# Attention score passes on one core: keys and queries fetched for several heads at once, shifts written by one DMA, their parts made on VectorE

## The chip, the cores and the metric

The kernel runs on one core of a Trainium2 chip. Its time is the device time of one execution in microseconds (us). Before the change it is 2822.1 us, the median of three runs (2809.25 to 2826.09). Lower is better.

A core has five engines that take their instructions in order and wait for each other through semaphores: TensorE (PE, with its weight loads listed as PEld), VectorE (DVE), ScalarE (ACT), GpSimd (POOL) and SyncE (SP). SP computes nothing here. It issues nearly all DMAs.

## The reference, cut to what matters

The input is `x` of shape 4 x 2048 x 256 in float32. Two pre-norm layers follow each other, each with attention and a feed-forward part. The change touches the attention of the second layer, which has 16 heads of 16 channels, rotary positions and a causal mask:

```
Q, K, V = (proj(W_Q), proj(W_K), proj(W_V))
Q = _apply_rope(Q, cos, sin)
K = _apply_rope(K, cos, sin)
scores = jnp.einsum('bhsd,bhtd->bhst', Q, K) / jnp.sqrt(jnp.float32(D_K))
causal = jnp.tril(jnp.ones((S, S), dtype=bool))
scores = jnp.where(causal[None, None], scores, -jnp.inf)
attn = jax.nn.softmax(scores, axis=-1)
out = jnp.einsum('bhst,bhtd->bhsd', attn, V)
```

The first layer's attention has one head of 64 channels. Its feed-forward part is one product with weights rounded to fp8. The second layer's feed-forward part mixes each token with the one before it and has three 256 x 256 products.

## The kernel before, in words

**Tiles.** The 4 x 2048 tokens are cut into 16 blocks of 512 tokens (`BLK`), four per sequence. The 16 heads are taken in 4 groups of 4 (`HG`). A round is one block of queries with one group: 64 rounds. For the block with place `qb` in its sequence a round runs over `qb + 1` blocks of keys, which makes 160 pairs of round and key block in all.

**Two score passes per round.** A head has 16 channels. Query and key are each split into a high and a low part, and four products of them are stacked, so that a score matmul contracts over 64 rows (`QR`), plus 12 rows (`SR`) for the shifts. Pass D (`d_head`, L1043) computes scores with queries on the output's partitions, and DVE takes the row maxima (L792, and L788 on the diagonal block, which adds the mask). Pass E (`e_head`, L1101) computes the transposed scores, and ACT takes the exponential (L1119). The row maximum is subtracted inside the matmul: its negative is split into three bf16 parts, which stand in the 12 extra rows of the query tile `q`; the extra rows of the keys' tile `ke` hold ones in the three rows of the head and zeros elsewhere. In pass D the extra rows of `kd` are zero. `values` (L1127) then multiplies the exponentials with the values.

**From the maxima to the shifts** (`shifts`). When the last D unit of a round is done, DVE reduces the maxima (L1058, tile `sm`), `bf16_parts` makes the three parts with four small operations on POOL (L747 to L750, tile `mp`), TensorE transposes them (L761), ACT copies the result into tile `m` (L766), and four DMAs, one for each head, write the 12 rows of `m` into the head's query tile (L1067). The first layer's attention uses `bf16_parts` too, 16 times, so that it runs 80 times.

**Where keys and queries come from.** `l1_qkv` writes rotated queries and keys to DRAM (L991). `fetch` (L949) loads one head of one block, 64 rows of 2 KB (128 KB), into a buffer: `kd` for pass D (6 buffers), `ke0` to `ke3` for pass E (2 for each place in the group), `q` for queries (12 buffers, which is three rounds). The value blocks `v1` are loaded by L1079.

**The order of the work.** It isn't written out by hand. `Plan.op` takes each operation with its engine, a cost in ns, and what it reads and writes; `Plan.run` is a list planner that gives every operation a start by these costs, picks the PSUM bank or buffer for each result, and emits the program in that order, for each engine. `LAT` is the delay that it adds when an operation on that engine needs the result of another engine. A DMA is planned with 500 ns of issue on SP, 1300 ns until it moves data, its own cost (390 for a key fetch) and 700 ns to the end. The pace of D against E is set by `target`, and the other layers' parts (`l0_attention`, `l0_ffn`, `l1_qkv`, `l1_out`, `l1_ffn`) fill in between by due times. SP takes its DMAs in that order too, so a DMA that waits for a buffer holds all DMAs behind it. All 8 PSUM banks are one class, `ps`. Where TensorE would idle at the beginning and the end, the planner puts `warm` matmuls (L1466) that keep its clock up.

**Costs in the plan that the change names.** The four operations of `bf16_parts` count 1080 ns on POOL. The mixing of tokens in `l1_ffn` (L1209, two per half) counts 661 ns on DVE.

Of the kernel before, what the change touches and what calls it, by code (L numbers as in the profile page):

```python
# [23 lines left out]
P = 128  # L24
C = 256
CK = C // P
BLK = 512
# [35 lines left out]
LAT = {"ACT": 38.0, "DVE": 38.0, "PE": 55.0, "POOL": 68.0, "SP": 60.0}  # L63
# [8 lines left out]
class Plan:  # L72
# [50 lines left out]
    def run(self, key):  # L123
# [54 lines left out]
        while len(done) < total:  # L178
# [75 lines left out]
            if e == "SP":  # L254
                eng_free[e] = s + 500.0
                begin = max(s + 1300.0, dma_end[0])
                dma_end[0] = begin + o.occ
                o.finish = begin + o.occ + 700.0
            else:
                eng_free[e] = s + o.occ  # L260
                o.finish = s + o.lat
# [6 lines left out]
            for b in o.bufs:  # L268
# [11 lines left out]
                if b.left == 0:  # L280
                    free[b.cls][b.slot] = b.end + 55.0
# [100 lines left out]
def seq_kernel(  # L382
# [45 lines left out]
        "kd": (6, [QR + SR, BLK], F32R),  # L428
        **{f"ke{h}": (2, [QR + SR, BLK], F32R) for h in range(HG)},
        "q": (12, [QR + SR, BLK], F32R),  # L430
# [54 lines left out]
    for z, t in enumerate(tiles["q"] + tiles["kd"]):  # L485
        (nc.vector.tensor_copy, nc.scalar.copy)[z % 2](t[QR : QR + SR, :], none)
# [53 lines left out]
    def ready_ke(h):  # L540
# [11 lines left out]
        for t in tiles[f"ke{h}"]:  # L552
            nc.gpsimd.tensor_copy(
                t[QR : QR + SR, :].rearrange("p (a n) -> p a n", n=P),
# [186 lines left out]
    def bf16_parts(nm, n, mp, view, s):  # L741

        def f():
# [3 lines left out]
            nc.gpsimd.tensor_copy(o(0), v3(v))  # L747
            nc.gpsimd.tensor_tensor(v3(r), v3(v), o(0), ALU.subtract)
            nc.gpsimd.tensor_copy(o(1), v3(r))
            nc.gpsimd.tensor_tensor(o(2), v3(r), o(1), ALU.subtract)  # L750
        def v3(a):
            return a.rearrange("p (t h) -> p t h", t=TT)
        op("POOL", 1080.0, f, r=[has["l0" if n == TT else "l1"]], rw=[nm], w=[mp], stream=s)
# [193 lines left out]
    def fetch(cls, name, what, i, head, s):  # L947
        b = buf(cls, name)
        op("SP", 390.0, lambda: nc.sync.dma_start(  # L949
            T_(b)[:QR, :].bitcast(F32),  # L950
            rot_t[what][i][head * 8 : head * 8 + 8].rearrange("d c n -> (d c) n")), r=[rot[what][i]], w=[b], stream=s,
           off=OFF_FETCH)
# [72 lines left out]
    def d_units(i, g, Qs):  # L1025
# [3 lines left out]
        for kb in range(qb + 1):  # L1029
            Ks = [fetch("kd", f"kd_{tag}_{kb}_{h}", "k", i - qb + kb, g * HG + h, now[0])  # L1030
                  for h in range(HG)]
            for t in range(TT) if kb < qb else reversed(range(TT)):
                u = Unit()
                u.kb, u.t, u.diag, u.w, u.mx = kb, t, kb == qb, BLK if kb < qb else (t + 1) * P, mx
                u.Ks, u.Qs, u.r = Ks, Qs, (i, g)
# [4 lines left out]
    def d_head(u, h, s):  # L1040

        def f():
            nc.tensor.matmul(  # L1043
                T_(u.banks[h])[:, : u.w], T_(u.Qs[h])[:, u.t * P : (u.t + 1) * P],
                T_(u.Ks[h])[:, : u.w], start=True, stop=True,
# [492 lines left out]
```

## Time and profile before

| | |
|---|---|
| median of three runs | 2822.1 us (2809.25 to 2826.09) |
| profiled execution | 2808.66 us, of it 2806.9 us span |
| mean granted clock of TensorE | 0.985 |
| busy: PE, DVE, ACT, POOL | 2739.7, 1945.0, 1638.8, 693.4 us |
| DMA | 417.33 MB, 49.6% of 16 engines' time in the queue that SP feeds |
| DMA issues on SP: kd, ke, q, shifts | 640, 640, 256, 256 |
| median length of one such issue | 546, 547, 588, 756 ns |

In the lists of groups a line gives the source line, engine, operation, written and read tiles with shapes, and the count; behind the first bar the busy time in us and the mean ns of one; behind the second the idle time of the engine just before them and what ended most of it. In the chain that ended last each step goes back to what released it. SPq and PEldq are the sequencers of SP and of TensorE's weight loads: they issue DMAs and wait for semaphores. Where a line has "min/median/max", these are ns.

### The profile page before, as it was taken

How to read it: one execution, taken by the hardware profiler on the slowest of the kernel's cores; microseconds unless marked ns; L12 is line 12 of the kernel's file. 1: busy time of each engine (PE TensorE's matmuls, PEld its weight loads, DVE VectorE, ACT ScalarE, POOL GpSimd, SP SyncE). 2: the span in 40 equal slices, each digit the busy share in tenths (PEclk: the TensorE clock that was granted, in tenths of full speed). 3: DMA queues.
4: the chain of work that ended last, by engine and by line, in shares of the span. 5: the costliest groups of instructions: out<-in, count | busy, mean ns of one | idle time of the engine just before them, and what ended most of it. 6: DMA issues, size and time to landing. Idle time of an engine off the chain costs nothing.

```text
span 2806.9 us, 47871 instructions
## 1 busy us (share of the span) xinstructions
PE 2739.7 (98%) x15447; PEld 1655.1 (59%) x15550; DVE 1945.0 (69%) x5040; ACT 1638.8 (58%) x3163; POOL 693.4 (25%) x955
## 2 busy tenths in 40 slices
PE   9999999999999999999999999999999999999998
PEld 5555665565656565655565656566565566555564
DVE  4567688787646778777674678867765477777871
ACT  3345566556565656656666456655666555655665
POOL 4551124013113313212113132501221422120000
PEclk9999999999999999999999999999999999999999
DMA  3664546444446564634544565644454645454331
GB/s 93 192 211 130 173 128 201 131 123 153 126 127 211 153 189 139 193 110 131 162 146 141 167 189 157 188 143 123 124 156 118 192 151 177 148 175 130 108 100 38
DMA packets 275291, 417.33 MB, mean 149 GB/s; under 512 B 42657, under 2 KB 108898, under 8 KB 275042
## 3 DMA queue, kind: packets, MB, share of 16 engines
q1 hardware_dynamic: 273568, 413.57, 49.6%
q8 instruction: 126, 2.06, 0.3%
q14 instruction: 123, 1.01, 0.1%
q10 hardware_dynamic: 1474, 0.69, 0.1%
HBM read 294.56 MB, written 100.66 MB: 141 GB/s over the span
## 4 chain that ended last, share of the span: by engine, by line
PE 81%; DMA 7%; DVE 5%; issue 2%; ACT 2%; POOL 2%; SPq 1%; POOLq 0%; ACTq 0%; DVEq 0%
PE ps L1043 18%; PE ps L1101 17%; PE ps L1127 16%; PE ps L708 9%; PE ps L715 6%; PE ps L894 3%; DMA kd<-k 3%; PE ps L798 2%; DVE mx L792 2%; PE ps L689 1%; DVE ps L788 1%; PE ps L882 1%; PE ps L850 1%; PE ps L903 1%; PE ps L851 1%
## 5 line engine op out<-in xcount | busy, mean ns | idle before, releaser
L1119 ACT ACTIVATE p<-ps 128x512 f32<-128x512 f32 (+1 forms) x2240 | 1188.9, 598 | 649.5 <-PE ps L1101 386.3
L792 DVE TENSOR_REDUCE mx<-ps 128x1 f32<-128x512 f32 x1632 | 1030.2, 683 | 285.1 <-PE ps L1043 260.7
L1043 PE MATMUL ps<-kd,q 76*128 76x512 f32 (+3 forms) x2560 | 1007.7, 419 | 26.3 <-DMA kd<-k 12.6
L1101 PE MATMUL ps<-q,ke 76*128 76x512 f32 (+3 forms) x2560 | 955.3, 401 | 12.6 <-DMA q<-m 3.8
L788 DVE CUSTOM_DVE_ANT_0 ps<-ps,dmask 128x128 f32<-128x128 f32 (+3 forms) x1088 | 507.1, 517 | 257.0 <-PE ps L1043 246.8
L1043 PEld LDWEIGHTS ps<-kd,q 76*128 76x128 f32 x2560 | 481.1, 193 | 246.8 <-issue 87.4
L1101 PEld LDWEIGHTS ps<-q,ke 76*128 76x128 f32 x2560 | 477.3, 191 | 200.3 <-issue 77.6
L1127 PE MATMUL ps<-p,v 128*32 128x512 f32 (+3 forms) x5120 | 541.6, 540 | 1.1 <-DVE mx L792 0.8
L1127 PEld LDWEIGHTS ps<-p,v 128*32 128x32 f32 x5120 | 135.0, 110 | 256.8 <-issue 235.0
L708 PE MATMUL ps<-wb,W 128*128 128x256 f32 x768 | 187.2, 388 | 0.2
L638 POOL TENSOR_SCALAR sm<-sm 128x4 f32<-128x4 f32 x64 | 15.4, 241 | 670.2 <-DVE sm L632 647.9
L798 PE MATMUL ps<-maskT_b,ident_b 128*128 128x128 bf16 (+2 forms) x721 | 177.7, 246 | 0.4
L708 PEld LDWEIGHTS ps<-wb,W 128*128 128x128 f32 x768 | 145.9, 194 | 24.0 <-ACT p L1119 1.0
L788 DVE DVE_READ_ACCUMULATOR2_ANT mx<- 128x1 f32 x1088 | 153.7, 141 | 0.0
L798 PEld LDWEIGHTS <-ident_b 128*128 128x128 bf16 x768 | 75.9, 99 | 120.5 <-issue 103.5
L894 PE MATMUL ps<-p,v 128*65 128x512 f32 (+3 forms) x320 | 145.0, 540 | 1.3 <-ACT p L889 0.7
L774 POOL TENSOR_TENSOR r<-w,r 128x512 fp32r<-128x512 f32 x80 | 103.4, 1296 | 107.0 <-DVE r L773 89.9
L660 ACT ACTIVATE w<-x,sm 128x256 f32<-128x256 f32 x192 | 105.6, 604 | 34.7 <-DVE sm L645 20.3
L979 POOL TENSOR_TENSOR w<-w,cs 128x512 f32<-128x512 f32 x64 | 86.3, 1348 | 158.9 <-ACT w L972 150.5
L889 ACT ACTIVATE p<-ps 128x512 f32<-128x512 f32 (+3 forms) x160 | 86.2, 540 | 67.2 <-PE ps L798 18.8
L738 POOL TENSOR_TENSOR x<-x,w 128x512 f32<-128x512 f32 x32 | 41.1, 1286 | 331.7 <-DVE w L1235 324.5
L715 PE MATMUL ps<-W,wa 128*128 128x512 f32 x256 | 121.8, 599 | 0.7 <-DMA wa<-in_wqk1T 0.5
(123 smaller groups left out, 2515.8 us busy)
## 6 DMA issues: line engine op xcount, KB each, us to landing
kd<-k SPq DMA_DIRECT2D x640, 128.0 KB
ke<-k SPq DMA_DIRECT2D x640, 128.0 KB
k<-r SPq DMA_DIRECT2D x128, 256.0 KB
q<-r SPq DMA_DIRECT2D x128, 256.0 KB
q<-q SPq DMA_DIRECT2D x256, 128.0 KB
v<-v SPq DMA_DIRECT2D x160, 136.0 KB
x<-mid SPq DMA_DIRECT2D x62, 256.0 KB
v<-vs SPq DMA_DIRECT2D x16, 544.0 KB
```

What stands on the lines that cost most here:

```text
L660: nc.scalar.activation(d, T_(x)[:, t, :], AF.Identity, bias=m[:, 16 + t : 17 + t], scale=m[:, 8 + t : 9 + t],)
L708: nc.tensor.matmul(dst, lhsT[:, k, t * P : (t + 1) * P], w[:, k, :], start=(k == 0), stop=(k == CK - 1),)
L715: nc.tensor.matmul(dst, w[:, k, c0 : c0 + P], xT[:, k, :], start=(k == 0), stop=(k == CK - 1))
L774: op("POOL", pool2(BLK), lambda: nc.gpsimd.tensor_tensor(T_(lo), T_(f32), T_(hi), ALU.subtract), r=[f32, hi], w=[lo], stream=s)
L788: nc.vector.tensor_tensor_reduce(a, a, dmask[:, BLK - w :], 1.0, LOW, ALU.add, ALU.max, out())
L792: nc.vector.reduce_max(out(), a, axis=AX.X)
L798: nc.tensor.matmul(o, ident_b, maskT_b[:, 0, :] if len(o.shape) == 2 else maskT_b[:, : o.shape[1], :], start=False, stop=True,)
L894: nc.tensor.matmul(T_(acc)[: D0 + 1, c0:], T_(V_)[:, kt % TT, :], T_(p)[:, c0:], start=(kt == 0), stop=(kt == nkt - 1),)
L1043: nc.tensor.matmul(T_(u.banks[h])[:, : u.w], T_(u.Qs[h])[:, u.t * P : (u.t + 1) * P], T_(u.Ks[h])[:, : u.w], start=True, stop=True,)
L1101: nc.tensor.matmul(T_(u.banks[j])[:, c : c + u.w], T_(u.Ks[h])[:, u.t * P : (u.t + 1) * P], T_(u.Qs[h])[:, u.c0 :], start=h % u.n == 0, st ...
L1119: op("ACT", act(u.n * u.w), lambda: nc.scalar.activation(T_(u.ps[j])[:, c0:], T_(u.banks[j])[:, c0:], AF.Exp, scale=DK**-0.5), r=[u.banks[ ...
L1127: nc.tensor.matmul(T_(acc)[h * 32 : (h + 1) * 32, u.c0 :], T_(u.V)[:, (u.t * HG + h) * VW : (u.t * HG + h) * VW + 32], T_(u.ps[h // u.n])[ ...
```

## The change

Per key block, pass D has two fetches of two heads each (`kd`: 3 buffers of two heads) where it had four of one, and pass E has one fetch of four heads (`ke`: 2 buffers of four heads). Queries come with one fetch of four heads (`q`: 3 buffers of four heads). The space that the buffers take is the same, and so are the bytes moved. The 12 shift rows go into all four heads' places by one DMA whose source is read four times. The four operations that make the parts run on DVE, planned at 320 ns. Some of the planner's constants differ: the delay towards TensorE is 165 instead of 55 and also counts when a PSUM bank comes free; a DMA issue counts 600, the time until it moves data 1900; a fetch counts 390 per head, the shift DMA 200; L1209 counts 950.

```diff
-LAT = {"ACT": 38.0, "DVE": 38.0, "PE": 55.0, "POOL": 68.0, "SP": 60.0}
+LAT = {"ACT": 38.0, "DVE": 38.0, "PE": 165.0, "POOL": 68.0, "SP": 60.0}
...
-                eng_free[e] = s + 500.0
-                begin = max(s + 1300.0, dma_end[0])
+                eng_free[e] = s + 600.0
+                begin = max(s + 1900.0, dma_end[0])
...
-                    free[b.cls][b.slot] = b.end + 55.0
+                    free[b.cls][b.slot] = b.end + (LAT["PE"] if b.cls == "ps" else 55.0)
...
-        "kd": (6, [QR + SR, BLK], F32R),
-        **{f"ke{h}": (2, [QR + SR, BLK], F32R) for h in range(HG)},
-        "q": (12, [QR + SR, BLK], F32R),
+        "kd": (3, [QR + SR, 2, BLK], F32R),
+        "ke": (2, [QR + SR, HG, BLK], F32R),
+        "q": (3, [QR + SR, HG, BLK], F32R),
...
-            nc.gpsimd.tensor_copy(o(0), v3(v))
-            nc.gpsimd.tensor_tensor(v3(r), v3(v), o(0), ALU.subtract)
-            nc.gpsimd.tensor_copy(o(1), v3(r))
-            nc.gpsimd.tensor_tensor(o(2), v3(r), o(1), ALU.subtract)
+            nc.vector.tensor_copy(o(0), v3(v))
+            nc.vector.tensor_tensor(v3(r), v3(v), o(0), ALU.subtract)
+            nc.vector.tensor_copy(o(1), v3(r))
+            nc.vector.tensor_tensor(o(2), v3(r), o(1), ALU.subtract)
...
-        op("POOL", 1080.0, f, r=[has["l0" if n == TT else "l1"]], rw=[nm], w=[mp], stream=s)
+        op("DVE", 320.0, f, r=[has["l0" if n == TT else "l1"]], rw=[nm], w=[mp], stream=s)
...
-    def fetch(cls, name, what, i, head, s):
+    def fetch(cls, name, what, i, head, n, s):
+
         b = buf(cls, name)
-        op("SP", 390.0, lambda: nc.sync.dma_start(
-            T_(b)[:QR, :].bitcast(F32),
-            rot_t[what][i][head * 8 : head * 8 + 8].rearrange("d c n -> (d c) n")), r=[rot[what][i]], w=[b], stream=s,
-           off=OFF_FETCH)
+        op("SP", 390.0 * n, lambda: nc.sync.dma_start(
+            T_(b)[:QR].bitcast(F32),
+            rot_t[what][i][head * 8 : (head + n) * 8].rearrange("(h d) c n -> (d c) h n", h=n)),
+           r=[rot[what][i]], w=[b], stream=s, off=OFF_FETCH)
...
-            Ks = [fetch("kd", f"kd_{tag}_{kb}_{h}", "k", i - qb + kb, g * HG + h, now[0])
-                  for h in range(HG)]
+            Ks = [fetch("kd", f"kd_{tag}_{kb}_{z}", "k", i - qb + kb, g * HG + 2 * z, 2, now[0])
+                  for z in range(2)]
...
-        for h in range(HG):
-            op("SP", 100.0, lambda h=h: nc.sync.dma_start(
-                T_(u.Qs[h])[rows, :].bitcast(F32), T_(m)[rows, :].bitcast(F32)),
-               r=[m], w=[u.Qs[h]], stream=s)
+        op("SP", 200.0, lambda: nc.sync.dma_start(
+            T_(u.Q)[rows].bitcast(F32),
+            T_(m)[rows, None, :].to_broadcast([SR, HG, BLK]).bitcast(F32)), r=[m], w=[u.Q], stream=s)
...
-            Ks = [fetch(f"ke{h}", f"ke_{tag}_{kb}_{h}", "k", i - qb + kb, g * HG + h, now[0])
-                  for h in range(HG)]
+            K = fetch("ke", f"ke_{tag}_{kb}", "k", i - qb + kb, g * HG, HG, now[0])
...
-                op("DVE", 661.0, lambda k=k, d=d, z=z: nc.vector.scalar_tensor_tensor(
+                op("DVE", 950.0, lambda k=k, d=d, z=z: nc.vector.scalar_tensor_tensor(
...
-            Qs = queries[i, g] = [
-                fetch("q", f"q_{i}_{g}_{h}", "q", i, g * HG + h, now[0]) for h in range(HG)]
+            Qs = queries[i, g] = fetch("q", f"q_{i}_{g}", "q", i, g * HG, HG, now[0])
```

The matmuls read the head's part of the wider tiles (`T_(u.K)[:, h, ...]`, `T_(u.Ks[h // 2])[:, h % 2, ...]`, `T_(u.Q)[:, h, ...]`). Below the changed lines the source lines move by one or two: L1043 becomes L1045, L792 L793, L788 L789, L761 L762, L747 to L750 become L748 to L751, L949 becomes L951, L1067 L1068, L1058 L1060.

More of the change, by code (lines that the diff above doesn't have):

```diff
@@ L484, in seq_kernel @@
     nc.vector.memset(none, 0.0)
-    for z, t in enumerate(tiles["q"] + tiles["kd"]):
-        (nc.vector.tensor_copy, nc.scalar.copy)[z % 2](t[QR : QR + SR, :], none)
+    for t in tiles["q"] + tiles["kd"]:
+        for h in range(t.shape[1]):
+            (nc.vector.tensor_copy, nc.scalar.copy)[h % 2](t[QR : QR + SR, h, :], none)
     wo0 = const.tile([D0 + 1, C + 1], F32, name="wo0")
@@ L551, in ready_ke @@
         )
-        for t in tiles[f"ke{h}"]:
+        for t in tiles["ke"]:
             nc.gpsimd.tensor_copy(
-                t[QR : QR + SR, :].rearrange("p (a n) -> p a n", n=P),
+                t[QR : QR + SR, h, :].rearrange("p (a n) -> p a n", n=P),
                 r[:, None, :].to_broadcast([SR, BLK // P, P]),
@@ L1034, in d_units @@
                 u.kb, u.t, u.diag, u.w, u.mx = kb, t, kb == qb, BLK if kb < qb else (t + 1) * P, mx
-                u.Ks, u.Qs, u.r = Ks, Qs, (i, g)
+                u.Ks, u.Q, u.r = Ks, Qs, (i, g)
                 u.banks = [bank(f"d_{tag}_{kb}_{t}_{h}") for h in range(HG)]
@@ L1043, in f @@
             nc.tensor.matmul(
-                T_(u.banks[h])[:, : u.w], T_(u.Qs[h])[:, u.t * P : (u.t + 1) * P],
-                T_(u.Ks[h])[:, : u.w], start=True, stop=True,
+                T_(u.banks[h])[:, : u.w], T_(u.Q)[:, h, u.t * P : (u.t + 1) * P],
+                T_(u.Ks[h // 2])[:, h % 2, : u.w], start=True, stop=True,
             )
-        o = pe(f, max(pass_(u.w), LOADS), end=pass_(u.w), r=[u.Qs[h], u.Ks[h]], w=[u.banks[h], u.mx], stream=s)
+        o = pe(f, max(pass_(u.w), LOADS), end=pass_(u.w), r=[u.Q, u.Ks[h // 2]], w=[u.banks[h], u.mx], stream=s)
         chain(("d", h), o)
@@ L1085, in e_units @@
                 u.w = BLK - u.c0
-                u.Ks, u.V, u.Qs = Ks, V, Qs
+                u.K, u.V, u.Q = K, V, Qs
                 u.first, u.last = kb == qb and t == 0, kb == kbs[-1] and t == TT - 1
@@ L1101, in f @@
             nc.tensor.matmul(
-                T_(u.banks[j])[:, c : c + u.w], T_(u.Ks[h])[:, u.t * P : (u.t + 1) * P],
-                T_(u.Qs[h])[:, u.c0 :], start=h % u.n == 0, stop=not u.diag,
+                T_(u.banks[j])[:, c : c + u.w], T_(u.K)[:, h, u.t * P : (u.t + 1) * P],
+                T_(u.Q)[:, h, u.c0 :], start=h % u.n == 0, stop=not u.diag,
             )
@@ L1111, in e_head @@
             occ, end = max(pass_(u.w), LOADS), pass_(u.w)
-        o = pe(f, occ, end=end, r=[u.Qs[h], u.Ks[h], has["ke"]], w=[u.banks[j], u.ps[j]], stream=s)
+        o = pe(f, occ, end=end, r=[u.Q, u.K, has["ke"]], w=[u.banks[j], u.ps[j]], stream=s)
         chain(("e", h), o)
```

## The prediction

> **What bounds the kernel now.** I read the page's first two parts first, then its chain, then its groups. The profiled execution took 2808.66 us: 2806.9 us of span and 1.8 us around it. The median of the runs shown, 2822.1, lies 13.4 us above it.
>
> ```profile
> PE 2739.7 (98%) x15447; PEld 1655.1 (59%) x15550; DVE 1945.0 (69%) x5040; ACT 1638.8 (58%) x3163; POOL 693.4 (25%) x955
> ...
> PE  9999999999999999999999999999999999999998
> ...
> PE 81%; DMA 7%; DVE 5%; issue 2%; ACT 2%; POOL 2%; SPq 1%; POOLq 0%; ACTq 0%; DVEq 0%
> ...
> L1043 PE MATMUL ps<-kd,q 76*128 76x512 f32 (+3 forms) x2560 | 1007.7, 419 | 26.3 <-DMA kd<-k 12.6
> L1101 PE MATMUL ps<-q,ke 76*128 76x512 f32 (+3 forms) x2560 | 955.3, 401 | 12.6 <-DMA q<-m 3.8
> ```
>
> TensorE is busy in every slice, and its visible idle time is 2806.9 - 2739.7 = 67.2 us. The change removes no matmul, so all it can gain is stall time, and all it can lose is new stall time. The two groups are the score passes that the change feeds: L1043 (for the row maxima, "D") and L1101 (for the exponentials, "E"). "Busy" hides some more stall: in the trace the starts of two such 512-column matmuls are 230 ns apart when nothing holds them, while one record lasts about 395 ns, so a hold of up to 165 ns leaves no idle time. The mean of the 512-column form, 453 ns at L1043 and 431 at L1101, shows that there are such holds.
>
> Next the answers for tile q (idle time of TensorE and of its weight loads, and what ended it) and for lines L1043 and L1101 (duration min/median/max in ns).
>
> ```profile
>   DMA kd<-k: 13.5, 21
> ...
>   DMA q<-m: 8.4, 21
> ...
>   DMA q<-q: 5.7, 11
> ...
>   DMA ke<-k: 5.0, 6
> ```
> ```profile
> L1043 PEldq EVENT_SEMAPHORE  x551: 51/51/1990, 121.3 to 2723.7; - x184
> ```
> ```profile
> L1101 PEldq EVENT_SEMAPHORE  x510: 51/51/2780, 149.1 to 2761.2; - x170
> ```
>
> TensorE waits for data 32.6 us in the first four rows. The last two rows are separate wait instructions on TensorE's sequencer: one stands ahead of an instruction that has more than one semaphore to wait for.
>
> **The change, part by part.** Where I count "PE work", I took the instructions of TensorE in the program's order, before and changed, and gave each its usual start-to-start time in this trace (230 ns for 512 columns of a score pass, 176 for 384, 1.85 us for the 16 records of a values block, and so on). The list of both programs gives the same matmuls; only 12 more clock-warming ones (222 to 234).
>
> *Key fetches of D (kd, 640 of 128 KB to 320 of 256 KB).* The number of buffers' bytes is the same, so what counts is the PE work between the last reader of a buffer and the first reader of its next contents. Before, it is under 3 us for 27 of 634 refills and under 4 us for 51; changed, for 1 and 21 of 317 (the planner's DMA lead went from 1300 to 1900). Adding up what is missing to a need of N us, once per key block, N = 3.0 gives 11.8 us and 3.25 gives 16.9 for the program before: the measured 12.6 to 13.5 us fit N = 3.1. That agrees with the landing marks: a kd fetch lands 2.9 us (median) after its issue. What a 256 KB fetch of this pattern needs is not in the trace. Nearest rows: 256 KB of w<-con land in 2.73 us, 256 KB of x<-mid in 4.32. So N lies between 2.9 and 4.5, and the changed stall between 1.7 and 26 us. I take +0.35 us (four more 2 KB packets per DMA engine, median 84 ns each), N = 3.45: 3 us. Gain 10 us, range 12 gained to 13 lost.
>
> A rule is weighed here: the Trainium skill, "DMA: Bandwidth & Descriptors", section "Anatomy of one DMA", gives about 2.0 us plus bytes / 436 GB/s, so that 256 KB would cost only 0.3 us more than 128 KB. By it the stall would be about 3 us, by the row of x<-mid, which lands 1.4 us after a kd fetch would, about 26.
>
> *Key fetches of E (ke, 640 to 160) and queries (q, 256 to 64).* PE work between use and reuse of a ke buffer is never under 7.5 us, before or changed, so the ke wait stays or goes (5.0 to 0; I count 0). For q, the smallest spacing goes from 1.5 us to 4.5; 544 KB (v<-vs) land in 3.96 us, 0.9 more than a q fetch's 3.03, so N is 4.0 and nothing waits. Gain 4 us of the 5.7, range 0 to 5.7.
>
> *The shifts (four q<-m issues to one).* The last round shows the cost, in the chain of waits and in the row of the line:
>
> ```profile
> 2737.87 0.19 SPq L1067
> 2738.05 0.05 issue
> 2738.11 0.77 SPq L1067
> 2738.87 0.05 issue
> 2738.93 0.71 SPq L1067
> 2739.64 0.04 issue
> 2739.68 2.07 DMA q<-m
> ```
> ```profile
> L1067 SPq DMA_DIRECT2D q<-m x256: 713/756/1503, 147.0 to 2739.7; - x128
> ```
>
> Head 3 is written three issues, 2.4 us, after head 0, while TensorE uses it some 1.4 us later: the last head decides. One issue with the same landing saves about 1 us in a round that is tight. PE work between the transposes of the shifts (L761) and the first E matmul is also a little wider (5th percentile 3.7 to 4.4 us). Gain 5 us of the 8.4. If the one issue takes as long as four (3.0 us), nothing is gained: range 0 to 8.4. SP issues 1184 DMAs less (some 0.55 us each, 0.76 for shifts: about 690 us of its time). That matters only through the waits above, since SP mostly waits for TensorE to free buffers.
>
> *Fewer semaphores for TensorE.* With one buffer for four heads only the first reader must wait for its DMA. Score matmuls with a DMA wait go from 1174 to 475, instructions with two or more waits from 1191 to 596. Price of one: the row says 51 ns of the sequencer, which runs ahead, so 0 to 51 ns, 0 to 30 us in all. Starts of neighbouring score matmuls with such a wait between them lie 20 to 27 ns further apart on average than those without. 595 x 20 is 12 us, some of it DMA wait that is counted above: gain 9 us.
>
> *Parts of the shifts on DVE instead of POOL (4 x 80 small operations).* On POOL they took 1.11 us from first start to last end. This is the last round:
>
> ```profile
> 2735.03 0.22 POOL L747 CAST mp<-sm 128x16 bf16<-128x16 f32 x1 [1.38 <-PE ps L1101]
> ...
> 2735.91 0.23 POOL L750 TENSOR_TENSOR mp<-sm,mp 128x16 bf16<-128x16 f32 x1
> 2736.20 0.26 PEld L761 LDWEIGHTS <-mp 128*76 128x76 bf16 x4 [0.55 <-POOL mp L750]
> ```
>
> The nearest DVE rows are L632 (128x2, 182 ns) and L1058 (128x16, 175 to 217), and a DVE operation that needs the one before starts 30 ns after its end (L631 to L632 in the tail). Four make about 0.8 us. The planner now counts 320 ns where it counted 1080, and has moved L761 up by about 0.6 us (smallest PE work from the last D matmul to L761: 1.8 to 1.26 us); the chain shrinks by 0.3 us plus the 0.3 us handover to POOL. So L761 waits as it does now: 0, give or take 3. But the next row maxima queue behind the parts: 0.8 us on DVE 80 times, of which 0.32 is planned, so up to 0.48 x 80 = 38 us if each delay reached TensorE through a late PSUM bank. DVE is 69% busy and about one reuse of a bank in ten has no slack: loss 4 us, range 0 to 38.
>
> *The planner's other constants.* A larger lead from an engine to TensorE (55 to 165) would pay if it moved matmuls away from banks just released. It did not: the PE work between two writes of a bank after a 512-column D matmul is 1470 ns at the 5th percentile and 2.96 to 2.98 us at the median, before and changed. I count 0. Switches between the fast and the four-pass matmuls go from 1685 to 1655; a score matmul's interval is 316 ns instead of 230 ahead of one: gain 3 us. In the tail, after the last E matmul, stand 63 warming matmuls instead of 53; those ahead of L715 (24 for 19, 214 ns each) and of the last L708 (4 for 1) delay real work: loss 1.5 us, range 0 to 2.
>
> **Sum:** -10 - 4 - 5 - 9 + 4 - 3 + 1.5 = -25.5 us, so 2783 us for the profiled execution, 0.9% less. On the median of 2822.1 this is **2797 us**.
>
> **Rivals.** (A) *Much faster*: the multi-wait instructions cost their whole 51 ns and the DMA waits vanish: -30 - 12 - 5.7 - 8.4 - 3 = -59, 2763 us. For it: means of 453 and 431 ns show holds that no idle time tells. Against it: the sequencer runs ahead, and most intervals with such a wait are the ordinary 230 ns. (B) *No change*: the larger fetch lands like x<-mid (+13 us) and eats the rest: about -25 + 23 = -2 us, 2820. For it: that row. Against it: w<-con, just as large, lands in 2.73 us. This is also the case in which the change only moves issue time on SP, whose queue is not what TensorE waits for. (C) *Slower*: DVE turns into the bound at the round boundaries. Each of the 80 sets of parts stands in DVE's order ahead of row maxima that free PSUM banks. If the four operations take 1.1 us as on POOL (0.78 more than planned) and TensorE feels all of it, 0.78 x 80 = 62 us are lost against the 29.5 of the other terms: +33 us, 2855. It turns the sign from 29.5 / 80 = 0.37 us of new stall per set. For it: D's matmuls wait for banks that DVE frees already (29.7 and 22.2 us of idle time in the answer for tile kd are ended by L792 and L788). Against it: DVE is idle 31% of the time.
>
> **How the numbers follow.** Forecast (15 to 40 us gained) 0.49, A 0.17, B 0.19, C 0.15. About 1% (28 us) is what a measurement of this kernel can tell from no change, since its three runs spread over 17 us; half of the forecast's band is beyond it. Faster: 0.25 + 0.17 = 0.42. Slower: 0.12, as C with only two thirds of its delay stays within 1%. Same: the other half of the forecast, B and the rest of C, 0.46. The range reaches from A (2763, and a few us less for runs as fast as the profiled one) past B to the middle between B and C: 2758 to 2836.
>
> **What would show it.** In the changed profile: idle time of the D matmuls ended by kd at about 3 us and by q at 0 to 2; q<-m idle under 4; some 600 multi-wait instructions on TensorE; one shift issue per round near 0.76 us; POOL about 90 us less busy; DVE's L748 to L751 near 0.8 us a set; TensorE's idle time near 45 us. I am wrong if kd's idle time is above 15 us, if weight loads of D and E wait longer for L793 and L789, or if the idle time falls and the span does not.

## The result and the profile after

| | before | after |
|---|---|---|
| median (range), us | 2818.36 (2809.25 to 2826.09) | 2856.07 (2853.68 to 2861.13) |
| profiled execution, of it span, us | 2808.66, 2806.9 | 2855.55, 2853.8 |
| mean granted clock of TensorE | 0.985 | 0.976 |
| TensorE idle, us | 67.3 | 89.5 |
| TensorE at half clock, us | 83.1 | 139.5 |

The ratio of after to before is 1.0137, with a 95% interval of 1.0101 to 1.0173. The changed kernel is slower by 38 us, where 25.5 us of gain were forecast. (A fourth run of the kernel before brings its median from 2822.1 to 2818.36.) One execution on record, the profiled one of e13 below, was disturbed from end to end (6651.3 us of span): its trace is not read, and the ratios leave such executions out.

These are the lines of the page after that answer to the first fence of the prediction: busy time, TensorE's slices and its granted clock, the engines' shares of the chain that ended last, and the two groups of the score passes.

```profile
PE 2764.3 (97%) x15562; PEld 1668.2 (58%) x15562; DVE 2015.7 (71%) x5360; ACT 1634.5 (57%) x3163; POOL 624.2 (22%) x635
...
PE   9899999999999999999999999999999999999999
...
PEclk9998999999999999999999999999999999999999
...
PE 79%; DVE 12%; DMA 5%; issue 1%; POOL 1%; ACT 1%; POOLq 0%; SPq 0%; DVEq 0%; ACTq 0%
...
L1045 PE MATMUL ps<-kd,q 76*128 76x512 f32 (+3 forms) x2560 | 995.2, 419 | 29.5 <-DMA kd<-k 19.0
L1101 PE MATMUL ps<-q,ke 76*128 76x512 f32 (+3 forms) x2560 | 963.1, 408 | 15.2 <-DVE mx L793 7.2
```

TensorE stands longer, and it is also *busy* 24.6 us longer with the same real matmuls. The clock explains the second. The trace lists the stretches in which TensorE is granted half its clock. Nearly all last a multiple of 3.4 us; of the 20 after, nine last 3.4 us and five 10.2. A matmul in such a stretch takes twice as long (the record of a 512-column matmul of D has a median of 775 ns there and of 397 elsewhere), so a stretch costs half its length. The span can then be split into idle time, half of the half-clock time, and a rest:

| | span | idle | half of half-clock time | rest |
|---|---|---|---|---|
| before | 2806.9 | 67.3 | 41.6 | 2698.1 |
| after | 2853.8 | 89.5 | 69.8 | 2694.6 |
| difference | +46.9 | +22.2 | +28.2 | -3.5 |

The same split of the profiled executions of the experiments (spans from 2761 to 2897 us) leaves rests between 2692 and 2704 us. What this change and its parts do is therefore in the columns of idle time and half clock, but for these 12 us. In the trace after, 16 of the 20 half-clock stretches begin during a stand of TensorE longer than 0.15 us or within 3 us of its end, times that make up 12% of the span. Five of them stand behind waits for kd, five behind waits for the shifts' parts, four behind row maxima and two behind q<-m. Stands longer than 1 us went from 17 (25.2 us) to 26 (47.5 us); 12 of the 26 have such a stretch behind them. That a stand brings the clock down is read from this neighbourhood; no run here changed the clock by itself. The profiled execution of before is also a lucky one, 9.7 us under its median, while that of after is within 1 us of its own: 72 runs of the kernel before, beside the experiments, had granted clocks from 0.974 to 0.988, with a median of 0.982. So part of the 28.2 us is this luck.

The stands: idle time of TensorE and of its weight loads, by what ended it (us, times), in the answers for tile q of the kernel after,

```profile
  DMA kd<-k: 23.1, 19
...
  DMA q<-m: 10.5, 6
```

and for the line of the transposes of the shifts, first before, then after:

```profile
  POOL mp L750: 24.1, 49
```
```profile
  DVE mp L751: 83.4, 102
```

kd went from 13.5 to 23.1 us instead of to 3, q<-m from 8.4 in 21 waits to 10.5 in 6, and the transposes wait 83.4 us for the parts made on DVE. TensorE's matmuls alone, without the weight loads, stand 27.7 us there in 43 waits.

One stand for kd shows how it comes about. First the DMA issues of SP (start, length, line), then the chain of waits, then busy time by stretch (length; busy and count of PE, PEld, DVE, ACT, POOL; clock; DMA share; GB/s), all of the kernel after:

```profile
2476.86 0.61 SPq L951 DMA_DIRECT2D ke<-k  x1
2477.52 0.61 SPq L951 DMA_DIRECT2D q<-q  x1
2480.72 0.32 SPq L1079 DMA_DIRECT2D v<-v  x1
2481.13 2.63 SPq L951 DMA_DIRECT2D kd<-k  x2
```
```profile
2481.09 0.04 PE ps L1101
2481.13 6.53 DMA kd<-k
2487.66 0.14 issue
2487.79 0.94 PE ps L1045 x3
```
```profile
2478.00:2484.00 6.00, 6.00 (x43) 3.30 (x42) 5.30 (x12) 4.76 (x10) 4.81 (x4) 1.00 0.95 195
2484.00:2490.00 6.00, 3.33 (x19) 2.11 (x22) 2.91 (x6) 2.35 (x6) 5.15 (x6) 0.92 0.95 256
2490.00:2498.00 8.00, 8.00 (x37) 3.64 (x31) 6.25 (x11) 2.35 (x5) 2.14 (x3) 0.85 0.13 26
```

A ke and a q fetch of 512 KB each go out 0.66 us apart. The kd fetch behind them takes 6.53 us, where 2.9 was usual for the smaller one before and 3.75 is the median after; the DMA engines are 95% busy from 2478 to 2490 us. TensorE stands 2.67 us of the second stretch, and the granted clock falls to 0.92 in it and to 0.85 in the third, in which TensorE is never idle.

The landing marks of all fetches go the same way. Medians from the start of the issue to the last completion mark, in us:

| | kd | ke | q | q<-m | v |
|---|---|---|---|---|---|
| before | 2.89 (128 KB) | 2.87 (128 KB) | 3.03 (128 KB) | 2.10 | 2.46 |
| after | 3.75 (256 KB) | 5.52 (512 KB) | 7.55 (512 KB) | 3.81 | 3.58 |

### The profile page after: what moved, and what is told of

Its sections match the earlier page's. It is cut to its first block, busy times and chain, and to the rows that moved or that the text cites. A ratio compares the mean times of both kernels' runs of the same rounds, so it can differ in the third digit from the quotient of the medians.

```text
span 2853.8 us, 45465 instructions
## 1 busy us (share of the span) xinstructions
PE 2764.3 (97%) x15562; PEld 1668.2 (58%) x15562; DVE 2015.7 (71%) x5360; ACT 1634.5 (57%) x3163; POOL 624.2 (22%) x635
## 4 chain that ended last, share of the span: by engine, by line
PE 79%; DVE 12%; DMA 5%; issue 1%; POOL 1%; ACT 1%; POOLq 0%; SPq 0%; DVEq 0%; ACTq 0%
PE ps L1101 17%; PE ps L1045 17%; PE ps L1127 16%; PE ps L709 8%; PE ps L716 6%; PE ps L895 4%; DVE ps L789 3%; DMA kd<-k 3%; DVE mx L793 3%; PE ps L799 2%; PE ps L690 1%; PE ps L883 1%; PE ps L1465 1%; PE ps L884 1%; PE ps L885 1%
## 5 line engine op out<-in xcount | busy, mean ns | idle before, releaser
L793 DVE TENSOR_REDUCE mx<-ps 128x1 f32<-128x512 f32 x1632 | 1028.7, 682 | 283.3 <-PE ps L1045 266.0
L1045 PE MATMUL ps<-kd,q 76*128 76x512 f32 (+3 forms) x2560 | 995.2, 419 | 29.5 <-DMA kd<-k 19.0
L1101 PE MATMUL ps<-q,ke 76*128 76x512 f32 (+3 forms) x2560 | 963.1, 408 | 15.2 <-DVE mx L793 7.2
L789 DVE CUSTOM_DVE_ANT_0 ps<-ps,dmask 128x128 f32<-128x128 f32 (+3 forms) x1088 | 506.2, 516 | 239.0 <-PE ps L1045 230.8
L1045 PEld LDWEIGHTS ps<-kd,q 76*128 76x128 f32 x2560 | 483.2, 193 | 250.7 <-issue 94.4
L1101 PEld LDWEIGHTS ps<-q,ke 76*128 76x128 f32 x2560 | 486.1, 195 | 200.3 <-issue 85.7
L1127 PE MATMUL ps<-p,v 128*32 128x512 f32 (+3 forms) x5120 | 552.3, 549 | 0.0
L799 PE MATMUL ps<-maskT_b,ident_b 128*128 128x128 bf16 (+2 forms) x768 | 200.6, 261 | 0.0
L981 POOL TENSOR_TENSOR w<-w,cs 128x512 f32<-128x512 f32 x64 | 86.7, 1355 | 301.1 <-ACT w L974 270.1
L789 DVE DVE_READ_ACCUMULATOR2_ANT mx<- 128x1 f32 x1088 | 152.2, 140 | 0.0
L775 POOL TENSOR_TENSOR r<-w,r 128x512 fp32r<-128x512 f32 x80 | 103.7, 1299 | 84.1 <-DVE r L774 71.3
```

The lines of the kernel that those rows point to most:

```text
L775: op("POOL", pool2(BLK), lambda: nc.gpsimd.tensor_tensor(T_(lo), T_(f32), T_(hi), ALU.subtract), r=[f32, hi], w=[lo], stream=s)
L789: nc.vector.tensor_tensor_reduce(a, a, dmask[:, BLK - w :], 1.0, LOW, ALU.add, ALU.max, out())
L793: nc.vector.reduce_max(out(), a, axis=AX.X)
L799: nc.tensor.matmul(o, ident_b, maskT_b[:, 0, :] if len(o.shape) == 2 else maskT_b[:, : o.shape[1], :], start=False, stop=True,)
L1045: nc.tensor.matmul(T_(u.banks[h])[:, : u.w], T_(u.Q)[:, h, u.t * P : (u.t + 1) * P], T_(u.Ks[h // 2])[:, h % 2, : u.w], start=True, stop=True,
L1101: nc.tensor.matmul(T_(u.banks[j])[:, c : c + u.w], T_(u.K)[:, h, u.t * P : (u.t + 1) * P], T_(u.Q)[:, h, u.c0 :], start=h % u.n == 0, stop ...
```

## The experiments

All times are medians in us; the ratio is against the kernel before on the same chip, whose median lay between 2818.5 and 2827.0 in the five groups of experiments. "kd" is the idle time of TensorE's matmuls ended by kd<-k, "half" the time at half clock, both of the profiled execution.

| run | time | ratio [95% interval] | idle | kd | half |
|---|---|---|---|---|---|
| after | 2856.07 | 1.0137 [1.0101, 1.0173] | 89.5 | 19.0 | 139.5 |
| e1, after, parts on POOL | 2857.39 | 1.0096 [1.0058, 1.0135] | 82.2 | 23.1 | 163.2 |
| e3, after, parts planned later | 2900.79 | 1.0248 [1.0185, 1.0312] | 93.2 | 26.2 | 196.9 |
| e4, after, old constants | 2903.34 | 1.0269 [1.0224, 1.0313] | 111.4 | 27.0 | 163.0 |
| e6, after, kd single | 2836.51 | 1.0049 [1.0022, 1.0075] | 78.6 | 11.4 | 122.0 |
| e7, after, ke single | 2801.17 | 0.9933 [0.9911, 0.9955] | 68.9 | 4.1 | 58.1 |
| e8, after, q and shifts single | 2846.07 | 1.0084 [1.0043, 1.0124] | 86.6 | 17.2 | 105.9 |
| e10, after, ke by four DMAs | 2802.73 | 0.9927 [0.9899, 0.9955] | 64.1 | 4.8 | 77.8 |
| e2, before, parts on DVE | 2837.87 | 1.0036 [1.001, 1.0061] | 89.4 | 11.0 | 78.9 |
| e13, before, both DMA figures | 2786.67 | 0.9866 [0.9826, 0.9906] | | | |
| e17, before, lead 1900 | 2808.21 | 0.9952 [0.9934, 0.997] | 53.9 | 10.4 | 113.1 |
| e18, before, issue 600 | 2796.07 | 0.9907 [0.9878, 0.9937] | 55.2 | 5.7 | 64.2 |
| e14, before, delay to TensorE | 2833.12 | 1.0045 [1.002, 1.007] | 76.2 | 27.4 | 138.3 |
| e15, before, mixing at 950 | 2819.34 | 0.9987 [0.9962, 1.0011] | 62.9 | 11.8 | 115.1 |
| **e5, before, all new constants** | **2773.32** | 0.9829 [0.9798, 0.986] | 38.1 | 4.5 | 59.5 |
| e9, e5 with ke for four heads | 2818.74 | 0.997 [0.9942, 0.9999] | 62.2 | 20.0 | 115.9 |
| e11, e5 with parts on DVE | 2794.18 | 0.9894 [0.9833, 0.9955] | 64.5 | 6.6 | 67.6 |
| e12, e5 with kd in pairs | 2788.95 | 0.9876 [0.9824, 0.9928] | 53.3 | 13.6 | 83.3 |
| e16, e5 with q and shifts | 2780.68 | 0.9851 [0.9815, 0.9888] | 46.9 | 6.1 | 74.2 |

The other three runs of e13 lie between 2784.7 and 2786.9. The groups ran on different chips, so a difference between runs of two groups is also given by their ratios where it matters, with 1% of the kernel before as 28 us. Every edit lets the planner place the whole program anew, so part of any difference can come from the new order rather than from the edit: e3, which changes one planned delay and no instruction, moved the time by 45 us.

### The parts on DVE

e1 puts the four operations back on POOL in the changed kernel, e2 moves them to DVE in the kernel before (the same lines the other way), and e3 leaves them on DVE but tells the planner that the result comes 2400 ns later.

```diff
-            nc.vector.tensor_copy(o(0), v3(v))
+            nc.gpsimd.tensor_copy(o(0), v3(v))
...
-        op("DVE", 320.0, f, r=[has["l0" if n == TT else "l1"]], rw=[nm], w=[mp], stream=s)
+        op("POOL", 1080.0, f, r=[has["l0" if n == TT else "l1"]], rw=[nm], w=[mp], stream=s)
```
```diff
-        op("DVE", 320.0, f, r=[has["l0" if n == TT else "l1"]], rw=[nm], w=[mp], stream=s)
+        op("DVE", 320.0, f, r=[has["l0" if n == TT else "l1"]], rw=[nm], w=[mp], stream=s, lat=2400.0)
```

> The changed kernel with the four operations that make the parts back on POOL (planned 1080 ns again), all else as changed. Theory 1 (the parts on DVE are what costs: TensorE stands at the transposes of the shifts, 27.7 us of idle time, and the clock is halved for some microseconds after long stands): about 2805 us, no idle time of TensorE before L762 worth naming, granted clock back at 0.985 or so. Theory 2 (the larger fetches land too late and hold the queue): about 2845 us, the kd idle time stays near 19 us. Theory 3 (the planner's other costs give a worse order): about 2850 us.

> The kernel before with one part of the change alone: the parts on DVE, planned 320 ns. Theory 1: about 40 us slower than the kernel before, with 20 to 30 us of idle time of TensorE before L761. Theory 2 and 3: no slower than 5 us.

> The changed kernel, parts on DVE, but the planner is told that their result comes 2400 ns after their start (instead of 402), so that the transposes stand about 2 us later in TensorE's order. Theory 1 (TensorE stands because the result is late, and not because DVE is taken up): the idle time before L762 goes from 27.7 to under 5 us, the time to about 2815 us. If DVE's time itself is what costs (row maxima queue behind slow parts): L762 stands no more but D's and E's matmuls wait longer for DVE, about 2845 us.

Measured: e1 2857.39, not to be told from after (by the ratios 12 us less, with intervals that overlap), although TensorE's matmuls stand only 4.5 us at the transposes instead of 27.7. kd rose from 19.0 to 23.1 and the half-clock time from 139.5 to 163.2. e2 took 2837.87, some 10 us more than before, with 32.5 us of stand at the transposes. e3 lost the stand too, and was 45 us slower than after (31 by the ratios): kd, q<-m and the half-clock time all rose. Neither of the two times expected came, and why its order is so much worse is open. So the stand is real, it has a price where the DMAs leave it one (e2), and it is not the main thing that made the changed kernel slow. With e1 the theory that the parts are the main cause fell.

Why the stand is there can be read in the trace. The rows of the four operations and of a reduction beside them, in the kernel after (ns min/median/max):

```profile
L748 DVE CAST mp<-sm x64: 172/186/1258, 142.8 to 2774.7; 128x16 bf16<-128x16 f32 x64
```
```profile
L749 DVE TENSOR_TENSOR sm<-sm,mp x64: 174/176/1182, 143.0 to 2774.9; 128x16 f32<-128x16 f32 x64
```
```profile
L1060 DVE TENSOR_REDUCE sm<-mx x64: 169/188/220, 142.6 to 2774.4; 128x16 f32<-128x16 f32 x16, 128x16 f32<-128x32 f32 x16, 128x16 f32<-128x48 f32 x16, 128x16 f32<-128x64 f32 x16
```

The medians are as forecast, but the longest are seven times as long, while the reduction never exceeds 220 ns. One case, in the order of time:

```profile
1536.90 1.50 POOL L981 TENSOR_TENSOR w<-w,cs 128x512 f32<-128x512 f32 x1
1537.20 1.25 DVE L748 CAST mp<-sm 128x16 bf16<-128x16 f32 x1
...
1538.37 1.25 POOL L775 TENSOR_TENSOR r<-w,r 128x512 fp32r<-128x512 f32 x1
1538.48 1.18 DVE L749 TENSOR_TENSOR sm<-sm,mp 128x16 f32<-128x16 f32 x1
1539.69 0.19 DVE L750 CAST mp<-sm 128x16 bf16<-128x16 f32 x1
1539.91 0.19 DVE L751 TENSOR_TENSOR mp<-sm,mp 128x16 bf16<-128x16 f32 x1
1540.16 0.42 PEld L762 LDWEIGHTS <-mp 128*76 128x76 bf16 x4 [2.51 <-DVE mp L751]
```

L748 ends at 1538.45, when POOL's L981 ends (1538.40); L749 ends at 1539.66, when POOL's L775 ends (1539.62). An operation on DVE of 0.18 us here stands until the running operation on POOL is through. Over the run, L748 takes 177 ns (median) while POOL is idle, and 781 ns in the 19 of 80 cases where a POOL operation runs. The Trainium skill, "SBUF — State Buffer", section "Who interferes with whom", states this: DVE and GpSimd share a pair of ports as an exclusive lock, which copies and casts can take and for which an operation with two SBUF inputs contends, while a reduction does not. The rows agree with it on all three kinds.

### The planner's constants

e4 gives the changed kernel the constants of before; e5 gives the kernel before the new ones and nothing else. These are e5's lines; e4's are the same the other way.

```diff
-LAT = {"ACT": 38.0, "DVE": 38.0, "PE": 55.0, "POOL": 68.0, "SP": 60.0}
+LAT = {"ACT": 38.0, "DVE": 38.0, "PE": 165.0, "POOL": 68.0, "SP": 60.0}
...
-                eng_free[e] = s + 500.0
-                begin = max(s + 1300.0, dma_end[0])
+                eng_free[e] = s + 600.0
+                begin = max(s + 1900.0, dma_end[0])
...
-                    free[b.cls][b.slot] = b.end + 55.0
+                    free[b.cls][b.slot] = b.end + (LAT["PE"] if b.cls == "ps" else 55.0)
...
-                op("DVE", 661.0, lambda k=k, d=d, z=z: nc.vector.scalar_tensor_tensor(
+                op("DVE", 950.0, lambda k=k, d=d, z=z: nc.vector.scalar_tensor_tensor(
```

> The changed kernel with the planner's constants of the kernel before (LAT of PE 55, 500 and 1300 ns for a DMA, 55 ns for a bank, 661 for L1209); fetches, shift DMA and parts as changed. Theory 1: the same as the changed kernel or slower, 2855 to 2880 us, as the transposes then stand 0.1 us earlier still. Theory 3 (the new constants cost): about 2820 us. Theory 2: slower, since refills of kd are again planned 1 us tighter, 2870 us with over 30 us of idle time ended by kd.

> The kernel before with the planner's new constants alone (LAT of PE 165, 600 and 1900 ns for a DMA, 165 ns until a PSUM bank is free, 950 for L1209); fetches of single heads, four shift DMAs, parts on POOL. Theory 2 (the larger fetches cost, the constants pay): 2790 to 2815 us, 10 to 35 us under the kernel before, with less idle time ended by kd (12.6 us before). Theory 3 (the new constants make the order worse): above 2835 us.

e4 is 47 us slower than after (37 by the ratios), e5 48 us faster than before. Both lie outside what any theory expected, e4 above and e5 below. The constants are worth about the same in both, and **e5, at 2773.32 us, beats both kernels**. Its idle time falls from 67.3 to 38.1 us, and the row of D's matmuls no longer names kd first:

```profile
L1043 PE MATMUL ps<-kd,q 76*128 76x512 f32 (+3 forms) x2560 | 995.9, 417 | 14.3 <-DMA q<-q 4.7
```

Five more runs take the constants apart; each has only its lines of the diff above: e13 the 600 and the 1900, e17 only the 1900, e18 only the 600, e14 the two lines with 165, e15 only the 950.

> The kernel before with only the planner's DMA figures new: 600 ns for an issue and 1900 until data moves. If these are what pays (key fetches are then planned earlier): 2770 to 2790 us, idle time ended by kd falls from 12.6 to under 7 us. If the delay towards TensorE pays: 2810 to 2830 us and kd idle time as before.

> The kernel before with one figure of the planner new: a DMA moves data 1900 ns after its issue instead of 1300. If this is what pays, since a matmul is then planned 0.6 us later behind its fetch: 2780 to 2795 us, idle time ended by kd under 7 us (12.6 before). If the issue's 600 ns pays, 2810 to 2825.

> The kernel before with the other figure new: SP is busy 600 ns with an issue instead of 500 (546 measured for a key fetch). If this pays, since the planner no longer packs issues closer than SP can make them: 2780 to 2800 us and a lower kd idle time. If the lead of 1900 pays, 2810 to 2825.

> The kernel before with only the delay towards TensorE new: 165 ns, and the same delay where a PSUM bank comes free. If it pays (matmuls planned away from results that have just come): 2775 to 2800 us with less idle time ended by DVE and ACT. If the prediction was right on this one constant: 2810 to 2830 us.

> The kernel before with only the token mixing planned at 950 ns. All theories: 64 operations whose planned length grows by 0.29 us, 2805 to 2830 us. Below 2800 it would be this constant that pays.

The two DMA figures pay, 1.3% together; each pays alone, the issue's 600 ns more (0.9%) than the lead (0.5%). e18 came out as the theory of the issue said, with less kd stand too; but the lead pays as well, so that it isn't the issue alone. The other two do not pay alone: 165 costs 0.5%, and 950 gives nothing that can be told from zero. Idle time of the D matmuls and weight loads ended by kd, in the answers for tile kd of e17, e18 and e14 in that order (13.5 before):

```profile
  DMA kd<-k: 11.4, 15
```
```profile
  DMA kd<-k: 6.4, 12
```
```profile
  DMA kd<-k: 28.5, 26
```

The new figures are nearer to what the trace shows. A kd issue keeps SP 546 ns (500 was planned), and a kd fetch lands 2.89 us after its issue, where the old plan had 1300 + 390 + 700 = 2390 ns and the new one has 2990. That the planner profits from a DMA cost that fits is the likely reason; it was not tried with other values. Whether 165 and 950 add anything on top of the DMA figures is open: the intervals of e13 and e5 overlap.

### The fetches, undone one at a time

In the changed kernel, e6 goes back to single kd fetches, e7 to single ke fetches, e8 to single query fetches and four shift DMAs. The readers of the tiles change with them.

```diff
-        "kd": (3, [QR + SR, 2, BLK], F32R),
+        "kd": (6, [QR + SR, 1, BLK], F32R),
```
```diff
-        "ke": (2, [QR + SR, HG, BLK], F32R),
+        **{f"ke{h}": (2, [QR + SR, 1, BLK], F32R) for h in range(HG)},
...
-            K = fetch("ke", f"ke_{tag}_{kb}", "k", i - qb + kb, g * HG, HG, now[0])
+            K = [fetch(f"ke{h}", f"ke_{tag}_{kb}_{h}", "k", i - qb + kb, g * HG + h, 1, now[0])
+                 for h in range(HG)]
```
```diff
-        "q": (3, [QR + SR, HG, BLK], F32R),
+        "q": (12, [QR + SR, 1, BLK], F32R),
...
-        op("SP", 200.0, lambda: nc.sync.dma_start(
-            T_(u.Q)[rows].bitcast(F32),
-            T_(m)[rows, None, :].to_broadcast([SR, HG, BLK]).bitcast(F32)), r=[m], w=[u.Q], stream=s)
+        for h in range(HG):
+            op("SP", 100.0, lambda h=h: nc.sync.dma_start(
+                T_(u.Q[h])[rows, 0, :].bitcast(F32), T_(m)[rows, :].bitcast(F32)),
+               r=[m], w=[u.Q[h]], stream=s)
```

> The changed kernel with the keys of pass D fetched one head at a time again (6 buffers of one head, 640 fetches of 128 KB). If the 256 KB fetch itself is what is late (landing 3.75 us against 2.89): kd's idle time from 19 to about 10 us and 2830 us. If the 512 KB fetches of ke and q in the same queue hold everything behind them: kd's landing and idle time stay as high, 2850 us.

> The changed kernel with the keys of pass E fetched one head at a time again (640 fetches of 128 KB instead of 160 of 512 KB). If the 512 KB fetches hold the queue: the values' loads land in 2.5 us again instead of 3.6, kd's in less than 3.75, the DMA queue's share falls from 55.8% towards 50%, half-speed time of TensorE from 139 us to about 100, 2825 us. If not: 2855 us.

> The changed kernel with queries fetched one head at a time and the shifts written by four DMAs again. If the one shift DMA and the 512 KB query fetch (landing 7.5 us) are what costs: q<-m waits of up to 3 us go, half-speed time falls by some 25 us, 2830 us. If ke is the cause: 2850 us.

Undoing ke alone gains 55 us and makes the kernel faster than before; the answer for tile kd then has

```profile
  DMA kd<-k: 5.2, 10
```

although kd still comes in pairs and ke ended no stand of TensorE's matmuls in the kernel after. Undoing kd alone gains 20 us. Undoing q and the shifts gains 10, with intervals that overlap. By the ratios the three gain 58, 25 and 15. The signs expected of e7 came only in part: half-clock time fell to 58.1 us, but the medians of the landings hardly moved (kd 3.82 us, v 3.06) and the queue's share only fell to 54.4%. What fell is the late end: nine kd fetches in ten land within 5.28 us instead of 6.01.

e10 keeps the ke tile for four heads and fills it with four DMAs of 128 KB, planned at 390 ns each, as the one was at 4 x 390.

```diff
-            K = fetch("ke", f"ke_{tag}_{kb}", "k", i - qb + kb, g * HG, HG, now[0])
+            K = buf("ke", f"ke_{tag}_{kb}")
+            for h in range(HG):
+                op("SP", 390.0, lambda h=h, K=K, j=i - qb + kb: nc.sync.dma_start(
+                    T_(K)[:QR, h, :].bitcast(F32),
+                    rot_t["k"][j][(g * HG + h) * 8 : (g * HG + h + 1) * 8].rearrange("d c n -> (d c) n")),
+                   r=[rot["k"][i - qb + kb]], w=[K], stream=now[0], off=OFF_FETCH)
```

> The changed kernel, its ke tile for four heads kept, but filled by four DMAs of 128 KB, one per head, instead of one of 512 KB. If the size of the one transfer is what hurts (packets of a small transfer wait behind 512 KB): near 2801, as with single ke buffers, kd idle time under 8 us. If what hurts is that one buffer for four heads comes free and is asked for all at once, so that 512 KB stand in the queue in a burst however they are cut: near 2856, kd idle time 15 us or more, and the last of the four fetches lands 5 us or more after the first is issued.

It takes 2802.73, like e7. The shared buffer is harmless; that the 512 KB go out in one DMA is what costs. And not because the four arrive sooner: from the first issue to the last landing a set takes 5.99 us (median) against 5.52 for the one DMA. The gain is with those behind. A kd fetch issued within 3.5 us behind a ke or q issue lands after 5.90 us in the kernel after (29 fetches) and after 4.47 in e10 (54; medians), a v fetch after 5.06 and 3.37. A likely reason, which no run tests, is SP's own issue time, 547 ns for each of the four: the packets go out spread, and fewer of them stand ahead when the next fetch is issued.

One rival is left. The plan counts 390 ns for each 128 KB more, while a landing grows by some 0.88 us for each (2.87 us for 128 KB, 5.52 for 512), an estimate from the medians above. Whether the one large DMA would still cost as much in an order planned with its true length, no run tried.

### The parts of the change on the new constants

e5 is the base here, and each run adds one part of the change to it: e9 the ke fetch for four heads, e12 kd in pairs, e11 the parts on DVE, e16 the query fetch and the one shift DMA, with the lines of the change's own diff.

> The kernel before with the new planner constants (2773 us in the run before this) and, of the change's other parts, only the one fetch of four heads for pass E. Theory (the 512 KB fetch holds SP's one DMA queue, small transfers behind it land late, and the clock falls after the stands): most of the 55 us that undoing it gave comes back, 2800 to 2830 us; idle time ended by kd above 10 us (4.5 without it), half-speed clock above 80 us (59.5), the kd landing median near 3.4 us (2.85). Rival (each part alone costs little, it is their meeting that costs): within 1% of 2773, kd idle time under 6 us.

> The kernel before with the new planner constants (2773 us) and the fetch of two heads at once for pass D. Theory (a 256 KB fetch needs some 0.9 us more than one of 128 KB, with the spacing of refills nearly the same): 2783 to 2800 us, idle time ended by kd 8 to 15 us (4.5 without it). Rival (pairs hurt only behind the 512 KB fetches of pass E): within 6 us of 2773, kd idle time under 6 us, kd landing median under 3.3 us.

> The kernel before with the new planner constants (2773 us) and the parts on DVE at 320. Theory (the parts stand behind POOL operations on DVE and are planned too short): 2783 to 2795 us, idle time of L761's weight loads ended by DVE 20 to 35 us, as in the two runs that had the parts on DVE. Rival (the stall only shows time that would be lost elsewhere, as undoing it in the changed kernel gave nothing): 2768 to 2780 us with the same stall.

> The kernel before with the new planner constants (2773 us) and the query fetch of four heads and the one shift DMA. Theory (512 KB in one transfer delays what is behind it, but only 64 times against 160 for ke; the one shift DMA lands later): 2780 to 2795 us, idle time of TensorE ended by q<-m 4 to 9 us. Rival (fewer shift issues help as predicted): 2764 to 2773 us, with q<-m idle time under 2 us.

The answers for tile kd of e5 and e9:

```profile
  DMA kd<-k: 4.7, 8
```
```profile
  DMA kd<-k: 21.5, 26
```

The ke fetch alone brings the kd stand back and 45.4 us with it (2818.74 - 2773.32; 40 by the ratios). In e9 kd fetches are as small as in e5. Those issued over 3.5 us behind a ke or q issue land as in e5 (2.78 and 2.76 us), those closer behind, 108 of 640, after 5.16 instead of 3.05. The median of all is 2.91 and not the 3.4 expected: the delay is with the few. The shift DMAs, which e9 leaves as they were, land after 4.71 us at the 90th percentile instead of 3.03, and the weight loads and matmuls wait 15.5 us for them:

```profile
  DMA q<-m: 15.5, 16
```

kd in pairs costs 15.6, the parts on DVE 20.9, queries and shifts 7.4. The four together make 89.3, so 2773.3 + 89.3 = 2862.6; the changed kernel, which has all of them and the constants, takes 2856.1. So the parts add up to within 7 us. By the ratios, e12, e11 and e16 cost 13, 18 and 6 us, and the sum ends 9 us under the changed kernel. The interval of e16 overlaps with that of e5, so its 7.4 us are not told from zero; those of e11 and e12 overlap with it at their ends, so that alone they are weak evidence (e6 and e2 point the same way).

The Trainium skill, "DMA: Bandwidth & Descriptors", section "Queues, rings and completion order", says that a DMA engine takes the descriptors of a ring in order, and that the increment which reports a DMA complete lands only after every earlier write of that engine. The landings behind 512 KB agree with that; which of the two holds a kd fetch up, no run here separates.

## Why the prediction was wrong, step by step

The forecast was 2797 us with a range to 2836; the time is 2856. Slower by over 1% had a chance of 0.12. Of the signs of being wrong, the first came: kd's stand of 19.0 us is above 15. The errors partly cancel: with the old constants the same change takes 2903 us (e4), so that the miss of 59 us is smaller than the one in the fetches and parts.

**The step that failed most is "the ke wait stays or goes (5.0 to 0; I count 0)".** A ke wait indeed ends no stand of TensorE's matmuls after. But the 512 KB of a ke fetch delay the kd, v and shift DMAs that SP issues behind it. I priced each fetch by its own reader and none by its neighbours in the one queue. The mis-sized term is 0, and it measured 45 us (e9) to 55 us (e7), 40 to 58 by the ratios.

*Key fetches of D.* I took N = 3.45 us for 256 KB and forecast 3 us of stand. The landing is 3.87 us even without large fetches of E (e12), and 3.75 after. The row of x<-mid (4.32) was the better guide than w<-con (2.73), and the weighed rule (the Trainium skill, "DMA: Bandwidth & Descriptors", section "Anatomy of one DMA", which gives it for DMAs issued by GpSimd, while these are SP's), which makes it 0.3 us longer than 128 KB, was too low by 0.6 to 0.7 us. Stand 19.0 for the matmuls instead of 3; 15.6 us of time lost on the new constants (e12), where a gain of 10 was counted.

*Queries.* "N is 4.0 and nothing waits": the fetch lands after 7.55 us, and after 5.75 in e16. The stand did fall, from 5.7 to 2.8, as the spacing is wide enough; what the transfer does to those behind it was left out here too.

*The shifts.* The count and the issue were right: one per round, 856 ns instead of the 760 expected.

```profile
L1068 SPq DMA_DIRECT2D q<-m x64: 837/856/1384, 146.9 to 2776.7; - x64
```

"One issue with the same landing" was not: the soonest lands after 3.26 us, where one of the four landed after 2.10 (median); the median after is 3.81. Even the bound that I kept, 3.0 us and nothing gained, was too good: the waits for q<-m went from 8.4 to 10.5 us.

*Fewer semaphores for TensorE.* The count was right:

```profile
L1045 PEldq EVENT_SEMAPHORE  x278: 51/51/372, 127.2 to 2762.7; - x139
```

It was 551, and at L1101 510 became 154. The gain of 9 us is not to be seen, nor ruled out: most of it would have to be in the rest of the split, which fell by 3.5 us, less than it varies between the other runs.

*Parts on DVE.* "Four make about 0.8 us" holds for the median set (0.84), but one set in ten takes over 2.3 us, because POOL holds DVE up, at which the row of L1209 in the trace of before hinted (720/744/1896 ns). "L761 waits as it does now" was wrong (24.1 to 83.4 us); the 4 us of loss were placed at the row maxima. Price alone: 10 us on before, 21 on e5. POOL got 69 us less busy, not 90.

*The planner's other constants.* "I count 0" was right for the one constant that I argued about, the delay towards TensorE (e14: 12 us slower, if anything). It was wrong for the set, 48 us: I used the lead of 1900 only inside the kd term and gave SP's 600 no term. The row that says 546 ns for an issue stood in my own table.

*The clock* has no term at all in the sum. It is 28.2 of the 46.9 us between the two profiled executions, some of it the luck of the first.

*The rivals.* B, a larger kd fetch that lands late, named the smaller part (15.6 us in e12) and priced it by its own stand alone; that a large fetch delays those behind it, no rival named. C said 2855, close to the time, but by another cause: DVE's parts in front of the row maxima. Stands of the score matmuls and their weight loads ended by row maxima went from 81.1 to 90.2 us only (29.7 + 22.2 + 20.7 + 8.5 before, 30.5 + 20.2 + 26.4 + 13.1 after), and without DVE's parts the time is the same (e1).

## What to carry to other kernels

Where all DMAs go through one queue, price a transfer by what is issued behind it as well as by its own reader: merge fetches only if nothing urgent follows within their landing time. A planner's cost that a trace can check (issue time, landing time) is worth checking first; here that alone beat both kernels. When TensorE is nearly always busy, a stand of 1 to 3 us should be priced with the half-clock time that may follow it (here behind 12 of 26), and an operation moved from GpSimd to VectorE with GpSimd's running operations.

## What was not expected of the hardware

- Four DMAs of 128 KB into one tile take 0.5 us longer than one of 512 KB (5.99 to 5.52), yet a 256 KB fetch behind them lands 1.4 us sooner (4.47 to 5.90).
- The packets of the same bytes take more of the DMA engines' time in the changed kernel. With the ke fetch in four DMAs again it is still 55.3% (e10), so the size of that DMA isn't all of it. The line of SP's queue (packets, MB, share of 16 engines' time), before and after:

```profile
q1 hardware_dynamic: 273568, 413.57, 49.6%
```
```profile
q1 hardware_dynamic: 255392, 413.50, 55.8%
```

- A 12-partition DMA whose source is read four times lands after 3.28 us (5th percentile, after), a plain one a fourth its size after 2.04 (the same, before).
- Half-clock time adds much to the price of stands, but not in proportion: half of it is 41.6 us beside 67.3 us of idle time before, 69.8 beside 89.5 after and 29.7 beside 38.1 in e5, yet 39.5 beside 89.4 in e2 and 56.6 beside 53.9 in e17.
- Small operations on DVE stand up to 1.1 us behind one on POOL, in two operations of the same set if POOL goes on without a break (L748 and L749 above: 2.43 us instead of 0.36).
